# Layer 0's values by seven products of halves, computed a batch ahead, with all experts merged through DRAM and the values' bias carried by the projection

## The chip, the cores and the metric

The kernel runs on one core of a Trainium2 chip. The metric is device time in microseconds (us), from one launch of the whole program. Before the change three runs took 2100.03, 2100.3 and 2100.56 us; the median is 2100.3. The engines are named as in the profile: PE (TensorE, matrix products), DVE (VectorE), ACT (ScalarE), POOL (GpSimd) and SP (SyncE, which here only issues DMAs). Each engine works through its own instructions in order.

## The reference

Two transformer layers in fp32 over x of shape 8 x 512 x 512 (batch, rows, width). What the change touches is the attention and the experts of layer 0 and one step of the attention of layer 1:

```python
# layer 0, attention: 16 heads of 32, causal
q = (x @ WQ_w.T + WQ_b)...; k = (x @ WK_w.T + WK_b)...; v = (x @ WV_w.T + WV_b)...
attn = softmax(where(causal, -inf, q k^T / sqrt(32)))
x = layernorm(x + (attn @ v) @ WO_w.T + WO_b)
# layer 0, experts: 8 experts, the top 2 of a router for each row
gup = x @ gate_up_proj + 2 * (x @ gup_lora_A^T) @ gup_lora_B^T
out = (silu(gate) * h) @ down_proj + 2 * (... @ down_lora_A^T) @ down_lora_B^T
x = layernorm(x + sum over the top 2 of weight * out)
# layer 1, attention: 8 heads of 64 in 2 groups, after an rms norm, not causal
x = layernorm(x + (softmax(q k^T / 8) @ v) @ Wo.T)
# layer 1, a quantised feed-forward layer, and a last layernorm
```

The weights of a softmax's row sum to one, so a constant added to all values of a head comes out of the attention as the same constant. That is why a bias of values can be added after the attention, as WV_b projected by WO_w.

## The kernel before, in words

The stages follow one another on PE: attention of layer 0 from about 5 to 685 us, the experts on tiles of routed rows to about 1060, attention of layer 1 to about 1603, the feed-forward layer to the end. A scheduler sets the order on each engine from its own estimates of durations, except where a stretch is held in the written order.

*Attention of layer 0* (`attention0`) loops over eight batches b of 512 rows. A batch has four groups g of four heads, and a group three units u: key tile 0, key tiles 1 and 3, key tile 2, whose scores are 512, 384 and 128, and 256 columns wide because of the causal mask. So a batch is twelve slots (g, u). In each slot PE makes the scores `sc` (one PSUM tile, so one at a time), then whatever `plan(b)` put into `todo` for the slot, then the weighted values `av` of the slot before (L1542), then the `late` thunks. ACT takes the exponent (L1503) and frees `sc`; POOL masks (L1513); DVE adds the unit to the group's running sum of p (L1550). After a group, PE sums over the keys (`rs`, L1557), ACT makes a first inverse from a logarithm and an exponent (`r_rough`, L78 and L79), DVE refines it (L80, L81) and multiplies (`aoT`, L1564).

The thunks are products of 128 x 512 outputs over four steps of 128, each step written as four pieces of 32 columns (`matmul_by_columns`, L67): the values `ps_v` of the batch itself, four of them in slots (0,0), (0,1) and (0,2), evicted by DVE with the bias added (L1396); the queries `ps_q` and keys `ps_k` of the next group; the projection `ps_o` of the batch before (L1425), its layernorm (L200 to L205), its turn and the router. All of these take PSUM tiles from one pool with two buffers that alternate strictly, so a product can start only when the one before the last has been evicted.

*Turning.* The normalised rows of batch b-1 are transposed in blocks of 32 by DVE (L108), written to DRAM by four stores (L113) and read back as `x1T` by one load (L116), all on SP. Loads that must not get ahead of that return are issued inside `behind_return()`: x of the next batch (L1353), its transpose xT (L1349, into one of two rooms that batches use in turn), and the merged experts' stores (L840) in group 3. SP's queue is in order, and its DMAs share 16 DMA engines. Late in the batch PE makes the router's logits (`score`, `ps_logits`, L515) from x1T; at the start of the next, `choose` (`ps_r`, then a chain of small DVE instructions, L534 to L565) picks the two experts of each row.

*Experts.* Each expert has six tiles of 128 x 512 weights. In unit u = 2 of batches 1 to 6 PE makes LoRA products into the free half of the scores' bank (`deltas`), ACT scales them (`scaled`, L827), and POOL adds them to the weights (`pair`). Experts 0 to 3 are loaded into SBUF at the start and merged there (k below 12, batches 1 to 3). Experts 4 to 7 are merged through DRAM (batches 4 to 6): a load of 256 KB (L837), POOL's add (L839), a store into `merged` (L840). Their room in SBUF holds the attention's weights and xT until the tiles begin; then `load(e)` brings them in.

*Attention of layer 1* forms the inverse of row sums in `normalise` with the same `inverse` (two steps of ACT and two of DVE), 32 times.

## Time and profile before

| what | before |
|---|---|
| median of three runs | 2100.3 us |
| profiled execution, its time | 2100.73 us |
| its span (first to last instruction) | 2098.9 us |
| granted clock of PE | 0.999 |
| PE busy | 2073.1 us (99%) |
| DVE, ACT, POOL busy | 1168.4, 670.6, 515.0 us |
| first scores of batches 0, 1, 2, 3 | 14.87, 82.87, 166.03, 250.50 us |
| first scores of batches 4, 5, 6, 7 | 334.97, 419.45, 503.92, 588.39 us |

In the lines of the profile "L1396 DVE TENSOR_TENSOR v<-ps_v,row" is an instruction of line 1396 on DVE that writes v from ps_v and row. In a timeline the first number is the start, the second the length of a run of equal instructions (x is their count), and in brackets is the idle time before it with what ended that. In a list of waits the numbers are the total, how often, and the longest. In a list of windows the columns are length, busy time of PE, its weight loads, DVE, ACT and POOL, then PE's clock, the share of the DMA engines' time, and GB/s. In a group of instructions they are busy time and mean ns of one, then the idle time before them and its cause. Pieces of a product run partly at the same time, so lengths of PE runs overlap, and the time between two starts is what a run costs.

### The profile page before, as it was taken

Reading aid. Unit: us, or ns where it says so; the run is one execution under the profiler, and the core shown is the slowest. Engines: PE = TensorE matmul, PEld = TensorE weight load, DVE = VectorE, ACT = ScalarE, POOL = GpSimd, SP = SyncE. Lnnn points to the kernel's source line nnn. Section 1 sums busy time; section 2 is a strip of 40 time slices with the busy share of each in tenths; the row PEclk is TensorE's granted clock in tenths of the full one; section 3 lists DMA queues with packets and bytes.
Section 4 is the critical chain, followed back from the end, with each engine's and each line's share of the span. In section 5 each row is a group of like instructions: output and inputs, shape, how many; then the busy total and the mean of one; then the engine's idle time right before and its main releaser. Section 6 shows DMA issues by size and latency. Waiting matters only on the chain. (4 is left out here: it accounts for less than half of the span.)

```text
span 2098.9 us, 36093 instructions
## 1 busy us (share of the span) xinstructions
PE 2073.1 (99%) x15074; PEld 1048.3 (50%) x15074; DVE 1168.4 (56%) x2028; ACT 670.6 (32%) x967; POOL 515.0 (25%) x509
## 2 busy tenths in 40 slices
PE   8999999999999999999999999999999999999998
PEld 2333333333334677774433333333335888888886
DVE  2556666766667633234146677766747644555444
ACT  2433434434434111111143433343332322222222
POOL 1343444434433221221053231323201000000000
PEclk9999999999999999999999999999999999999999
DMA  9011304325233568876431332233102311111000
GB/s 326 22 44 60 101 12 121 117 74 153 82 102 108 173 198 254 245 225 202 149 102 51 121 107 84 71 101 101 41 1 71 101 41 61 61 61 61 20 21 22
DMA packets 182093, 213.42 MB, mean 102 GB/s; under 512 B 72586, under 2 KB 126090, under 8 KB 178850
## 3 DMA queue, kind: packets, MB, share of 16 engines
q1 hardware_dynamic: 169280, 172.85, 26.3%
q0 software_dynamic: 10560, 34.61, 5.7%
q10 hardware_dynamic: 2082, 3.56, 0.6%
q8 instruction: 122, 2.00, 0.4%
q14 instruction: 49, 0.40, 0.1%
HBM read 132.58 MB, written 78.40 MB: 101 GB/s over the span
## 5 line engine op out<-in xcount | busy, mean ns | idle before, releaser
L1503 ACT ACTIVATE p<-sc 128x2048 f32<-128x2048 f32 (+1 forms) x96 | 152.4, 1588 | 157.9 <-PE sc L67 157.9
L1513 POOL TENSOR_SCALAR_AFFINE_SELECT p<-p 128x512 f32<-128x512 f32 x128 | 98.6, 782 | 338.6 <-ACT p L1503 328.0
L1246 DVE SCALAR_TENSOR_TENSOR hT<-ps_u,vec,sg 128x512 f32<-128x512 f32 x88 | 65.5, 745 | 189.6 <-PE ps_u L1241 189.4
L1257 PE MATMUL ps_f<-ffn_w,h_half 128*128 128x512 f32 x664 | 167.7, 393 | 2.7 <-DVE h_half L1252 1.9
L974 PE MATMUL ps_gu<-xrT,experts 128*128 128x256 f32 x736 | 166.6, 379 | 0.0
L1550 DVE TENSOR_TENSOR p<-p 128x1536 f32<-128x1536 f32 (+2 forms) x96 | 144.2, 1503 | 37.5 <-POOL x L1523 31.4
L1094 POOL TENSOR_TENSOR g_total<-g_total,r_inv 128x512 f32<-128x512 f32 x64 | 88.4, 1381 | 291.3 <-DVE r_inv L81 291.3
L974 PEld LDWEIGHTS ps_gu<-xrT,experts 128*128 128x128 f32 x736 | 139.3, 190 | 35.9 <-issue 19.0
L1893 ACT ACTIVATE p<-sc 128x1024 f32<-128x1024 f32 x128 | 124.2, 1016 | 85.6 <-PE sc L67 82.7
L1257 PEld LDWEIGHTS ps_f<-ffn_w,h_half 128*128 128x128 f32 x664 | 122.9, 188 | 34.4 <-DVE h_half L1252 7.3
L1241 PE MATMUL ps_g<-x_high,ffn_w 128*128 128x512 f32 x352 | 137.2, 390 | 0.0
L1241 PE MATMUL ps_g<-x_low,ffn_w 128*128 128x512 f32 x352 | 137.0, 389 | 0.0
L1241 PE MATMUL ps_u<-x_low,ffn_w 128*128 128x512 f32 x352 | 136.9, 389 | 0.0
L1241 PE MATMUL ps_u<-x_high,ffn_w 128*128 128x512 f32 x352 | 136.9, 389 | 0.0
L67 PE MATMUL sc<-qT,kT 64*64 64x512 f32 x1024 | 124.7, 602 | 2.6 <-ACT qT L1784 2.3
L67 PE MATMUL ps_q<-experts 128*32 128x512 f32 x1024 | 121.7, 604 | 5.0 <-DMA experts<-in_xT 4.7
L1244 ACT ACTIVATE sg<-ps_g,vec 128x512 f32<-128x512 f32 x88 | 60.6, 688 | 193.7 <-PE ps_g L1241 193.7
L67 PE MATMUL ps_v<-experts 128*32 128x512 f32 x1024 | 120.9, 595 | 0.0
L1912 PE MATMUL av<-p,v 128*64 128x512 f32 x512 | 120.8, 593 | 0.0
L202 POOL TENSOR_SCALAR rstd<-mv 128x4 f32<-128x4 f32 x15 | 3.9, 260 | 459.0 <-DVE mv L201 459.0
L67 PE MATMUL ps_o<-attn_out,aoT 128*64 128x512 f32 x512 | 116.4, 598 | 0.0
L67 PE MATMUL ps_k<-experts 128*32 128x512 f32 x1024 | 116.3, 594 | 0.0
(284 smaller groups left out, 3329.0 us busy)
## 6 DMA issues: line engine op xcount, KB each, us to landing
results<-y SPq DMA_DIRECT2D x68, 256.0 KB
pair<-xrT SPq DMA_DIRECT2D x30, 512.0 KB
xrT<-pair SPq DMA_DIRECT2D x120, 128.0 KB
turned<-turned SPq DMA_DIRECT2D x56, 256.0 KB
x<-in_x SPq DMA_DIRECT2D x8, 1024.0 KB
rows<-x SPq DMA_DIRECT2D x32, 256.0 KB
experts<-in_xT SPq DMA_DIRECT2D x7, 1024.0 KB
x<-rows SPq DMA_DIRECT2D x14, 512.0 KB
```

The costliest lines, as they stand in the source:

```text
L67: nc.tensor.matmul(out[m], lhsT=lhsT[:, m], rhs=rhs, start=start, stop=stop)
L974: nc.tensor.matmul(ps[:, j, :], lhsT=w, rhs=xT[:, c, :], start=c == 0, stop=c == ND - 1)
L1094: self.nc.gpsimd.tensor_tensor(self.total, self.total, r_inv, ALU.add)
L1241: nc.tensor.matmul(ps, lhsT=w[:, ts(dc, P)], rhs=x[:, dc, :], start=(dc, i) == (0, 0), stop=(dc, i) == (ND - 1, 1))
L1244: nc.scalar.activation(sg, g, AF.Silu, scale=vec[:, V_SG + c : V_SG + c + 1])
L1246: nc.vector.scalar_tensor_tensor(hT, u, vec[:, V_SU + c : V_SU + c + 1], sg, ALU.mult, ALU.mult)
L1257: self.nc.tensor.matmul(os[t], lhsT=h[:, ts(t, P)], rhs=self.weights(2 * NHID + c), start=(c, i) == (0, 0), stop=(c, i) == (NHID - 1, 1))
L1503: nc.scalar.activation(p, sc[:, :, :width], AF.Exp, scale=scale)
L1513: select = nc.gpsimd.affine_select(out=first, in_=first, pattern=[[0, 4], [1, P]], compare_op=ALU.is_ge, fill=0.0, base=0, channel_multipl ...
L1550: nc.vector.tensor_tensor(total[:, :, P * kt :], total[:, :, P * kt :], p[:, :, at : at + w], ALU.add)
L1893: nc.scalar.activation(p, sc, AF.Exp, scale=scale)
L1912: nc.tensor.matmul(st["av"][HD * j : HD * (j + 1), :], lhsT=st["v"][:, kt, HD * j : HD * (j + 1)], rhs=p[:, j, :], start=kt == 0, stop=kt ...
```

## The change

- **Values.** Batch 0 makes its values as before, without the bias. From batch 1 on a batch's 512 x 512 values are made from seven products of 256 x 256 blocks in place of eight (`ps_1of7` to `ps_7of7`, `seven`). This takes sums of blocks of the weights, formed once in batch 0 (`seven_of_weights`), sums of blocks of xT, formed by DVE in each batch (`seven_of_rows`, L806 of the changed kernel), and additions as the products are evicted (L1437 of the changed kernel, one or two per product). Six of the seven are put into slots of the batch before, (1,0) to (3,2), and the last into (0,0) of the batch itself. The values alternate between two rooms in the space of experts 2 and 3.
- **Row sums.** Those of xT(b+1) are in `late` of slots (0,2) and (1,0) of batch b. They read what `load_xT(b+1)` brings.
- **Bias.** `bias_v` is loaded by 4-byte elements, spread by DVE over an identity-shaped tile, projected once by `wo` in batch 0 and added to the row that POOL adds to x.
- **Experts.** All eight are merged through DRAM, in batches 1 to 6; the eight loads of experts 0 to 3 at the start go. Merged experts are loaded in batches 6 and 7, expert 3 after the last weighted values.
- **Layer 1.** `normalise` uses one DVE reciprocal in place of the four steps; a preload of ACT's table between two small activations goes with it.

```diff
--- before.py
+++ after.py
@@ -781,30 +781,49 @@
         return xn, [dev[:, 1, t : t + 1] for t in range(NT)]
 
 
+def seven_of_weights(nc, w, s):
+
+    def block(i, j):
+        return w[:, 2 * j : 2 * (j + 1), 256 * i : 256 * (i + 1)]
+
+    def sums(last):
+        for out, a, b, op in ((block(1, 0), block(0, 0), block(1, 0), ALU.subtract),) if last else (
+                (s[:, 0], block(1, 0), block(1, 1), ALU.add), (s[:, 1], s[:, 0], block(0, 0), ALU.subtract),
+                (s[:, 2], block(0, 1), s[:, 1], ALU.subtract)):
+            nc.vector.tensor_tensor(out, a, b, op)
+
+    return {1: block(0, 0), 2: block(0, 1), 6: s[:, 1], 5: s[:, 0], 7: block(1, 0), 3: s[:, 2], 4: block(1, 1)}, sums
+
+
+def seven_of_rows(nc, xT, t):
+
+    def block(i, j):
+        return xT[:, 2 * i : 2 * (i + 1), 256 * j : 256 * (j + 1)]
+
+    def sums(last):
+        for out, a, b in ((t[3], block(1, 1), block(0, 1)), (t[2], block(1, 0), t[1])) if last else (
+                (t[0], block(0, 1), block(0, 0)), (t[1], block(1, 1), t[0])):
+            nc.vector.tensor_tensor(out, a, b, ALU.subtract)
+
+    return {1: block(0, 0), 2: block(1, 0), 6: t[1], 5: t[0], 7: t[3], 3: block(1, 1), 4: t[2]}, sums
+
+
 class Experts:
 
 
 
     def __init__(self, env, pool, dram):
         self.env, self.nc = env, env.nc
-        self.merged = dram.tile([P, 4, EXPERT], F32, name="merged")
+        self.merged = dram.tile([P, E, EXPERT], F32, name="merged")
         self.w = pool.tile([P, E * EXPERT], F32, name="experts")
         self.by_expert = self.w.rearrange("p (e f) -> p e f", f=EXPERT)
 
-    def room(self, i):
-
-        at = 4 * EXPERT + i * ND * 512
-        return self.w[:, at : at + ND * 512].rearrange("p (u f) -> p u f", f=512)
+    def room(self, at, n):
+
+        return self.w[:, at : at + n * 512].rearrange("p (u f) -> p u f", f=512)
 
     def load(self, e):
-        at = e * EXPERT
-        if e >= 4:
-            self.nc.sync.dma_start(out=self.by_expert[:, e, :], in_=self.merged[:, e - 4, :])
-            return
-        for src, n in ((self.env.ins.gate_up[e], ND), (self.env.ins.down[e], UPS - ND)):
-            self.nc.sync.dma_start(out=self.w[:, at : at + n * 512].rearrange("p (u f) -> p u f", f=512),
-                                   in_=src.rearrange("u p f -> p u f"))
-            at += n * 512
+        self.nc.sync.dma_start(out=self.by_expert[:, e, :], in_=self.merged[:, e, :])
 
     def load_lora(self, pool, i):
 
@@ -825,15 +844,12 @@
         e, f = 2 * i, slice(512 * c + 256 * half, 512 * c + 256 * (half + 1))
         scaled = own.tile([P, 2, 256], F32, tag=f"scaled{i}", name="scaled")
         nc.scalar.mul(scaled, ps[:, e : e + 2, :], LORA_SCALE)
-        if not second:
-            w = self.by_expert[:, e : e + 2, f]
-            return {1 + i: lambda: nc.gpsimd.tensor_tensor(w, w, scaled, ALU.add)}
-        w = []
+        w, e = [], 4 * second + e
 
         def load():
             w.append(own.tile([P, 2, 256], F32, tag=f"merged{i}", name="merged"))
             ins, u = self.env.ins, c if c < ND else c - ND
-            src = (ins.gate_up if c < ND else ins.down)[4 + e : 6 + e, u, :, 256 * half : 256 * (half + 1)]
+            src = (ins.gate_up if c < ND else ins.down)[e : e + 2, u, :, 256 * half : 256 * (half + 1)]
             nc.sync.dma_start(out=w[0], in_=src.rearrange("e p f -> p e f"))
 
         return {0: load, 1 + i: lambda: nc.gpsimd.tensor_tensor(w[0], w[0], scaled, ALU.add),
@@ -1324,6 +1340,7 @@
     HD = 32
     scale = 1.0 / math.sqrt(HD)
     UNITS = ((0,), (1, 3), (2,))
+    ORDER = 1, 6, 2, 5, 3, 7, 4
     with ExitStack() as phase:
         work = phase.enter_context(tc.tile_pool(name="a_work", bufs=1))
         small = phase.enter_context(tc.tile_pool(name="a_small", bufs=2))
@@ -1334,14 +1351,21 @@
 
 
         nc.scalar.preload_act_table_set(EXP_AND_LN)
-        wv, wq, wk, wo = (experts.room(i) for i in (0, 2, 3, 5))
+        wv, x_odd, wq, wk, x_even, wo = (experts.room(4 * EXPERT + ND * 512 * i, ND) for i in range(6))
+        v_rooms = [experts.room(i * EXPERT, ND) for i in (2, 3)]
+
+        def quarters(at, n):
+            return experts.w[:, at : at + n * 512].rearrange("p (s u f) -> p s u f", s=n, f=256)
+
+        sv, t_x, t_last = (quarters(at, n) for at, n in ((EXPERT, 3), (EXPERT + 1536, 3), (2 * EXPERT + ND * 512, 1)))
+        t_x = [*(t_x[:, i] for i in range(3)), t_last[:, 0]]
 
         def load_w(room, i, units=slice(0, ND)):
             src = ins.w_attn0[ND * i + units.start : ND * i + units.stop]
             nc.sync.dma_start(out=room[:, units, :], in_=src.rearrange("u p f -> p u f"))
 
         def load_xT(b):
-            xts[b] = experts.room((1, 4)[b % 2])
+            xts[b] = (x_odd, x_even)[b % 2]
             if b == 0:
                 for c in range(ND):
                     nc.sync.dma_start(out=xts[b][:, c, :], in_=ins.xT[b][ts(c, P), :])
@@ -1363,6 +1387,8 @@
         nc.sync.dma_start(out=row, in_=ins.rows.partition_broadcast(P))
         load_w(wq, 1, others)
         load_w(wk, 2, others)
+        bias_v = own.tile([P, ND], F32, name="bias_v")
+        nc.sync.dma_start(out=bias_v, in_=ins.rows[0].rearrange("(c p) -> p c", p=P))
         router = Router(env, keep, routes, small, work, dram)
         router.load()
         load_x(0)
@@ -1372,13 +1398,10 @@
             nc.sync.dma_start(out=router.results[ts(i, P), :], in_=guard.total)
         load_w(wo, 3)
         experts.load_lora(work, 0)
-        for e in range(4):
-            experts.load(e)
 
         ones = own.tile([P, HD], F32, name="ones")
         nc.gpsimd.memset(ones, 1.0)
 
-        vs = [None] * NT
         heads = {}
         aoTs = {}
 
@@ -1392,8 +1415,55 @@
             ps = mm([P, D], "ps_v")
             for c in range(ND):
                 multiply(ps, xts[b][:, c, ts(t, P)], wv[:, c, :], c)
-            vs[t] = own.tile([P, D], F32, tag=f"v{t}", name=f"v{t}")
-            nc.vector.tensor_tensor(vs[t], ps, row[:, 0, :], ALU.add)
+            nc.vector.tensor_copy(v_rooms[b % 2][:, t, :], ps)
+
+        v_of, v_sums = seven_of_weights(nc, wv, sv)
+
+        def row_sums(b):
+            return seven_of_rows(nc, xts[b], t_x)
+
+        def seven(b, n):
+            x_of, _ = row_sums(b)
+            room = v_rooms[b % 2]
+            ps = mm([P, 2, 256], f"ps_{n}of7")
+            for s in range(2):
+                for k in range(2):
+                    matmul_by_columns(nc, ps[:, s, :], x_of[n][:, k, ts(s, P)], v_of[n][:, k, :], start=k == 0, stop=k == 1)
+
+            def block(i, j):
+                return room[:, 2 * j : 2 * (j + 1), 256 * i : 256 * (i + 1)]
+
+            def add(out, a):
+                nc.vector.tensor_tensor(out, ps, a, ALU.add)
+
+            if n == 1:
+                nc.scalar.copy(block(0, 0), ps)
+            elif n == 6:
+                add(block(1, 0), block(0, 0))
+            elif n == 2:
+                add(block(0, 0), block(0, 0))
+            elif n == 5:
+                add(block(1, 1), block(1, 0))
+            elif n == 3:
+                add(block(0, 1), block(1, 1))
+            elif n == 7:
+                add(block(1, 1), block(1, 1))
+                add(block(1, 0), block(1, 0))
+            else:
+                add(block(1, 0), block(1, 0))
+
+        spread = []
+
+        def spread_bias():
+            spread.append(work.tile([P, ND, P], F32, tag="logits", name="spread"))
+            for c in range(ND):
+                nc.vector.tensor_scalar(spread[0][:, c, :], env.ident, 0.0, bias_v[:, c : c + 1], ALU.mult, ALU.add)
+
+        def out_of_bias():
+            ps = mm([P, D], "ps_bias")
+            for c in range(ND):
+                multiply(ps, spread[0][:, c, :], wo[:, c, :], c)
+            nc.vector.tensor_tensor(row[:, 1, :], ps, row[:, 1, :], ALU.add)
 
         def query(b, g):
             ps = mm([P, S], "ps_q")
@@ -1540,7 +1610,7 @@
                 w = S - P * kt
                 for j in range(4):
                     nc.tensor.matmul(av[HD * j : HD * (j + 1), P * kt :],
-                                     lhsT=vs[kt][:, P * g + HD * j : P * g + HD * (j + 1)], rhs=p[:, j, at : at + w],
+                                     lhsT=v_rooms[b % 2][:, kt, P * g + HD * j : P * g + HD * (j + 1)], rhs=p[:, j, at : at + w],
                                      start=u == 0, stop=kt == UNITS[-1][-1])
                 at += w
             at = 0
@@ -1577,8 +1647,14 @@
         def plan(b):
 
             todo, late = ({(g, u): [] for g in range(ND) for u in range(len(UNITS))} for _ in range(2))
-            for slot, places in (((0, 0), (0, 1)), ((0, 1), (3,)), ((0, 2), (2,))):
-                todo[slot] += [lambda t=t: value(b, t) for t in places]
+            if b == 0:
+                for slot, places in (((0, 0), (0, 1)), ((0, 1), (3,)), ((0, 2), (2,))):
+                    todo[slot] += [lambda t=t: value(b, t) for t in places]
+                late[1, 0] += [lambda: v_sums(False), spread_bias]
+                todo[1, 1].append(out_of_bias)
+                late[1, 1].append(lambda: v_sums(True))
+            else:
+                todo[0, 0].append(lambda: seven(b, ORDER[-1]))
             pb, last = b - 1, b == NB - 1
             by_dma = 0 <= pb < by_blocks
             for g in range(ND):
@@ -1601,6 +1677,12 @@
                     todo[(3, 0) if last else (2, 2)].append(lambda: choose(pb))
             if b == 0:
                 todo[1, 0].append(lambda: router.merge_lora(mm([P, ND, E], "ps_wr")))
+            if b + 1 < NB:
+                for slot, last_sums in (((0, 2), False), ((1, 0), True)) if b else (((2, 1), False), ((2, 2), True)):
+                    late[slot].append(lambda last_sums=last_sums: row_sums(b + 1)[1](last_sums))
+                for n, slot in zip(ORDER, ((1, 0), (2, 0), (2, 2), (3, 0), (3, 1), (3, 2)) if b else
+                                   ((3, 0), (3, 0), (3, 1), (3, 1), (3, 2), (3, 2))):
+                    todo[slot].append(lambda n=n: seven(b + 1, n))
             if b > 1:
                 todo[0, 0].append(lambda: choose(b - 2, mm=aside))
                 todo[1, 0].append(lambda: dispatch(b - 2))
@@ -1649,8 +1731,12 @@
                         load_x(b + 1)
                 if b == NB // 2 and g == 0:
                     experts.load_lora(work, 1)
+                if b == NB - 2 and g == 1:
+                    with behind_return():
+                        experts.load(0)
                 if b == NB - 1 and g == 1:
-                    experts.load(4)
+                    for e in (1, 2, 4):
+                        experts.load(e)
                 if b == NB - 1 and g == 2:
                     order.enter_context(in_order(tc))
                 if b == NB - 1 and g == 3:
@@ -1672,6 +1758,7 @@
                 summing = lambda b=b, g=g, acc=acc: normalise(b, g, acc)
         waiting()
         summing()
+        experts.load(3)
         heads_ctx.close()
         tiles.open(tiles_ctx)
         tiles.open_rows()
@@ -1839,12 +1926,9 @@
 
         def prepare_table(function):
             out = work.tile([P, 2, S], F32, tag="p", name="p1_none", bufs=4)
-            return nc.scalar.activation(out[:, 0, :1], env.neg_half[:, :1], function)
-
-        with env.tc.issue_after(prepare_table(AF.Copy).ins):
-            preload = nc.scalar.preload_act_table_set(EXP_AND_LN)
-        with env.tc.issue_after(preload.ins):
-            prepare_table(AF.Exp)
+            nc.scalar.activation(out[:, 0, :1], env.neg_half[:, :1], function)
+
+        prepare_table(AF.Exp)
 
         small = env.small
         pieces = {0: self.first}
@@ -1920,7 +2004,7 @@
                 nc.tensor.matmul(rs[HD * j : HD * (j + 1), :], lhsT=ones, rhs=total[:, j, :], start=True, stop=True)
             r_inv = work.tile([P, S], F32, tag="r_inv", name="r_inv1")
             guard.watch_sums(rs, r_inv)
-            inverse(nc, r_inv, rs, work.tile([P, S], F32, tag="r_rough", name="r_rough1"))
+            nc.vector.reciprocal(r_inv, r_inv)
             ao = state[b]["aoT"][:, g, :]
             if b != self.BY_TENSOR:
 

```

## The prediction

> **What bounds the kernel now.** I read the page first (busy shares and the slices), then what TensorE (PE) waited for, then the stretches, and then the timelines of PE, SP, DMA, GpSimd (POOL) and VectorE (DVE) around the turn from one batch of layer 0 to the next. The page:

> ```profile
> PE 2073.1 (99%) x15074; PEld 1048.3 (50%) x15074; DVE 1168.4 (56%) x2028; ACT 670.6 (32%) x967; POOL 515.0 (25%) x509
> PEclk9999999999999999999999999999999999999999
> ```

> PE is the bound at full clock (0.999). Its longest waits, and columns for one early-merge batch (SBUF), one later batch (merged by way of DRAM) and attention of layer 1:

> ```profile
> PE ps_q L67 <- DMA experts<-in_xT: 4.7, 1, 4.7
> PE sc L67 <- ACT qT L1784: 2.3, 1, 2.3
> PE ps_f L1257 <- DVE h_half L1252: 1.9, 7, 0.5
> ```

> ```profile
> 250.50:334.97 84.47, 84.33 (x1080) 28.08 (x1080) 55.25 (x110) 33.94 (x44) 37.33 (x36) 1.00 0.22 67
> 419.45:503.92 84.47, 84.33 (x1080) 28.08 (x1080) 55.25 (x110) 33.93 (x44) 36.40 (x36) 1.00 0.37 115
> 1060.00:1603.00 543.00, 539.59 (x3271) 181.83 (x3269) 365.25 (x511) 213.26 (x315) 152.75 (x132) 1.00 0.25 75
> ```

> PE work removed is time gained, and any new wait of PE is time lost. The two batches last equally long with either way of merging.

> **The change part by part.** All by the profiled execution (2100.73 us; the median is 2100.3, 0.4 less, so I add the sum to the median).

> *Seven products.* The prices come from PE's timeline at the turn from batch 4 to batch 5, counted from 0 (start, length):

> ```profile
> 405.15 3.64 PE L67 MATMUL ps_q<-experts 128*32 128x512 f32 x32
> 408.60 0.61 PE L1542 MATMUL av<-p,v 128*32 128x256 f32 x8
> 409.15 1.12 PE L67 MATMUL sc<-q,k 32*64 32x384 f32 x32
> 410.20 3.64 PE L67 MATMUL ps_k<-experts 128*32 128x512 f32 x32
> 413.65 1.04 PE L1542 MATMUL av<-p,v 128*32 128x512 f32 x8
> 414.51 1.04 PE L1557 MATMUL rs<-p,ones 128*32 128x512 f32 x8
> 415.49 0.69 PE L67 MATMUL sc<-lora 16*64 16x256 f32 x16
> ```

> By starts, a full product (ps_q; ps_v is the same form) takes 3.45, four steps of 0.86. A step of 512 columns is 0.86 where the next has the same tile shape (413.65 to 414.51) and 0.98 where it changes (to 415.49), so a change of shape is 0.12. The step of 256 columns takes 0.55 with a change: 0.43. Half the width is half the time, and 0.55 is no bound, because a seventh follows and precedes products of its own shape. A seventh is four such steps, 1.72. Seven are 12.05 against 4 x 3.45 = 13.8: -1.72 a batch, batches 1 to 7. Batch 0 keeps its four values.

> *A small stall filled.* The first scores of a batch (419.45 here) wait for ACT's second `scaled` to read the scores' bank; it ended at 334.92 a batch earlier, the scores began at 334.97. PE's last weighted values would have let them begin 1.03 earlier. The last seventh now stands there: -1.03 more. So a batch without new stalls is 84.47 - 2.75 = 81.72.

> *Unstalled sum.* From the start of batch 0's scores to batch 1's, 68.0 us: + 3.45 (bias through the projection, one product) + 6 x 1.72 (sevenths of batch 1) - 0.9 (its own filled stall) = +12.9. Batch 1: -2.8. Batches 2 to 6: 5 x -2.75 = -13.75. Batch 7 drops 13.8 and keeps one seventh: -12.07; its queries then follow a choose chain on DVE, +1.25. Together -14.5.

> *The new wait.* This decides. The row sums of x(b+2) need its load, and DVE works in order. The order of the built kernel puts two of those sums (L806, the first waiting for that load's semaphore) on DVE right behind the eviction of product 5, and ahead of product 3's eviction, the sums of p, r_inv, aoT, products 7 and 4 and the whole choose chain, in each of the turns 1 to 2 up to 5 to 6. Before, nothing waited early for xT. SP issues the load behind x1T's return, x and two stores:

> ```profile
> 409.50 0.33 SPq L116 DMA_DIRECT2D x1T<-turned  x1
> 409.92 0.39 SPq L1353 DMA_DIRECT2D x<-in_x  x1
> 410.37 1.37 SPq L840 DMA_DIRECT2D merged<-merged  x2
> 411.78 0.48 SPq L1349 DMA_DIRECT2D experts<-in_xT  x1
> ```

> and the 16 DMA engines, in 40 slices of 404 to 426 us, are full until about 423.5:

> ```profile
> DMA  9899989710094599898699799999999999600000
> ```

> The load's last semaphore update is at 423.43, 13.9 after x1T's issue (13.4 a batch later; 11.6 to 11.7 in batches without stores, which now all have them). Call the start of the last group's scores, 404.10, zero. Before, x1T was issued at +5.4; products 6 and 2 move in front and take 3.44 of PE from after to before that point, while 6's eviction (0.65) delays the normalised rows, so it comes 2.8 to 3.1 earlier: +2.3. POOL's merges (3.50, ending before the stores) still fit. The load lands at L = +15.8 (15.3 to 16.7, from 13.4 to 13.9 and the two issue offsets). DVE reaches it at +7.15 (scores 1.05, the query product 3.45, product 5 1.72, and 0.93 until that is evicted: 0.69 and the lag seen on others). It waits 8.6.

> Queued behind, after L: two sums and product 3's eviction (3 x 0.69), done at L+2.1; p, r_inv, aoT, p at L+8.1; 7 (twice), 4, two row sums at L+11.4; the choose chain, 6.08 here:

> ```profile
> 428.23 0.18 DVE L534 TENSOR_REDUCE red<-ps_r 128x4 f32<-128x32 f32 x1
> 434.91 0.68 DVE L1396 TENSOR_TENSOR v<-ps_v,row 128x512 f32<-128x512 f32 x1
> 436.43 0.75 DVE L1407 TENSOR_SCALAR q<-ps_q,vec 128x512 f32<-128x512 f32 x1 [0.84 <-PE ps_q L67]
> ```

> then q's eviction, which ends at L+18.7. The two PSUM buffers of the products alternate: ps_logits needs product 3 evicted (L+2.2 against PE's arrival at +15.87, so 2.1), and the next ps_k needs q evicted (against +30.48, so L+18.75-30.48 = L-11.7). The first stall is contained in the second. At L = 15.8 that is 4.1, with POOL and DVE slowing each other up to 4.6: 4.3, range 3.4 to 5.5. Were xT never late, DVE's own chain would still cost 1.3. Five turns: 5 x 4.3 = +21.5. In turn 0 to 1 xT lands at 72 to 75, its sums come at 85: nothing.

> [...]

> *More DVE work.* Four evictions become seven plus four row sums: +7 x 0.69 = 4.8 on 55.25 of 84.47 busy. Its cover is that idle time; its cost where the cover is gone is in the chain above. ACT gets a copy of 0.6 on 33.9: nothing.

> *Merging all by DRAM.* 24 more loads and stores on SP and DMA (share 0.22 to 0.37, as later batches have). The equal 84.47 says 0, bar the 2 us later landing, already in L. Eight start loads (6 MB) go, so xT(1) is issued near 21 and not 36 us: nothing waits for it. The last loads of merged experts lie 37 us ahead of first use, landing in about 8: 0.

> *bias_v.* 512 packets of 4 bytes ahead of the router's loads, against r_wr (512 of 32 bytes), landed 14.7 to 16.5. DVE's spread waits for it near 16, the first value's eviction is due at 19.6: 0, up to 1 if it lands later; below 0 no row allows.

> *Attention of layer 1.* ACT's two steps and DVE's two become one reciprocal:

> ```profile
> L80 DVE SCALAR_TENSOR_TENSOR r_inv<-r_inv,r_rough 128x512 f32<-128x512 f32 x63 | 43.6, 692 | 117.6 <-ACT r_rough L79 116.7
> L1561 DVE RECIPROCAL r_inv<-r_inv 128x512 f32<-128x512 f32 x1 | 3.3, 3340 | 0.0
> ```

> DVE: 3.34 - 0.69 - 0.73 = +1.92, 32 times, 61 on 365.25 of 543. It starts 1.2 earlier, as DVE idles 1.87 a time for ACT's r_rough. aoT comes 0.7 later where DVE is idle, 1.9 where it is dense; the projection reads it a group or more later. Bounds 0 and 8 x 0.69 = 5.5 (one exposed per batch); I take 0. The table switch is reordered, its total kept: 0.

> Sum: -14.5 + 21.5 = **+7.0, 2107.3**.

> **The rivals.**
> 1. *xT is in time* (issued earlier or moved faster than the rows have it). [...] Against: engines full from 410 to 423.5. L below 13 gives s = 1.3: -14.5 + 6.5 = -8, **2092.3**, faster. It decides at s = 2.9, L = 14.4 to 14.6.
> 2. *Half late*, L about 14.4, s = 2.7: -14.5 + 13.5 = -1, **2099.3**, no difference.
> 3. *The reciprocal binds in layer 1.* For: 26.91 of the 30 us from 1266 to 1296 are busy on DVE. Against: 67% over the stage. +5.5 on the forecast: **2112.8**.

> **How the numbers follow.** Forecast 0.5 (s of 3.4 to 5.5 gives 2102.5 to 2113.3), rival 1 0.2, rival 2 0.17, rival 3 0.13. Measurement tells 0.2%, 4.2 us. Faster is rival 1 with the edge of 2: 0.21; same is 2 and the forecast's low edge: 0.20; slower the rest: 0.59. The range cuts a tenth at each end: 2091 to 2115.

> **What the profile would show.** Right: DVE waits of about 8 us five times for experts<-in_xT at the row sums; PE waiting for DVE at ps_logits and ps_k about 2 each in five batches; batches of 86 us in place of 84.5; 49 sevenths of 1.72; no wait of PE in layer 1 that leads to the 32 reciprocals of 3.34. Wrong: batches near 82 to 83 (xT in time), a seventh above 1.8, or waits of ps_o for aoT after 1060 us.

## The result

The changed kernel takes 2114.61 us (median of five runs, 2111.25 to 2119.06) against 2100.48 (2100.03 to 2101.4): slower by a factor of 1.0069, 95% interval 1.005 to 1.0087. The forecast was slower, at 2107.3 with a range of 2091 to 2115. The sign and the mechanism came true; the loss is twice the forecast, +14.1 for +7.0.

### The profile after

PE's longest waits in the changed kernel. The first two lines are new:

```profile
PE ps_k L67 <- DVE q L1477: 16.0, 6, 3.3
PE ps_logits L515 <- DVE experts L1437: 6.6, 5, 2.1
PE ps_q L67 <- DMA experts<-in_xT: 4.4, 1, 4.4
```

22.6 us of waiting for DVE, where the prediction summed five stalls of 4.3 and one of 1.25 to 22.75. What holds DVE, in its own list of waits:

```profile
DVE experts L806 <- DMA experts<-in_xT: 40.2, 5, 8.8
```

Five waits of 8.0 on average (8.6 predicted). The turn from batch 4 to 5 on the three engines, SP first, then DVE (the row sums, product 3, the queries' eviction), then PE:

```profile
418.79 0.33 SPq L116 DMA_DIRECT2D x1T<-turned  x1
419.22 1.22 SPq L1377 DMA_DIRECT2D x<-in_x  x1
420.49 1.02 SPq L856 DMA_DIRECT2D merged<-merged  x2
421.55 0.54 SPq L1373 DMA_DIRECT2D experts<-in_xT  x1
```

```profile
433.33 1.42 DVE L806 TENSOR_TENSOR experts<-experts 128x512 f32<-128x512 f32 x2 [8.14 <-DMA experts<-in_xT]
434.67 0.68 DVE L1437 TENSOR_TENSOR experts<-ps_3of,experts 128x512 f32<-128x512 f32 x1
...
452.59 0.74 DVE L1477 TENSOR_SCALAR q<-ps_q,vec 128x512 f32<-128x512 f32 x1
```

```profile
435.40 1.06 PE L515 MATMUL ps_logits<-x1T,r_wr 128*32 128x512 f32 x8 [1.43 <-DVE experts L1437]
436.29 1.91 PE L67 MATMUL ps_7of<-experts 128*32 128x256 f32 x32
...
453.38 5.34 PE L67 MATMUL ps_k<-experts 128*32 128x512 f32 x32 [3.27 <-DVE q L1477]
458.53 1.05 PE L1612 MATMUL av<-p,experts 128*32 128x384 f32 x16
```

The last group's scores start at 418.02. x1T is issued 0.8 later (2.3 predicted), xT's load lands 15.3 later (15.8 predicted; the profile has its last semaphore update at 433.31), and the sums start at once. The query's eviction ends at +35.3, and ps_k starts there. So far the mechanism is the predicted one. The new thing stands in the third and fourth line: ps_k, a full product, takes 5.15 from start to start and not 3.45. PE's granted clock in the windows around it:

```profile
450.87:454.28 3.41, 0.90 (x11) 0.30 (x15) 3.21 (x10) 2.04 (x4) 0.64 (x1) 1.00 0.00 0
454.28:457.70 3.42, 3.42 (x24) 0.86 (x20) 3.25 (x5) 0.00 (x0) 0.44 (x1) 0.50 0.01 2
457.70:461.11 3.41, 3.41 (x52) 1.10 (x48) 1.93 (x2) 1.05 (x2) 3.41 (x3) 1.00 0.02 5
```

For 3.41 us PE runs at half clock, right behind a stretch in which it was busy for only 0.90 us, and loses half of that, 1.7 us. The profile has four such stretches, from 174.39, 276.79, 365.54 and 454.29, beside one behind PE's last work, which every profile here has; the profile before has none but that. Two whole batches, 5 and 6, show the price:

```profile
438.99:527.08 88.09, 83.60 (x1180) 31.29 (x1177) 59.81 (x117) 34.43 (x44) 37.75 (x34) 0.98 0.39 127
527.08:612.18 85.10, 81.83 (x1180) 30.96 (x1177) 59.97 (x117) 34.43 (x44) 37.91 (x35) 1.00 0.34 101
```

Batch 6 is 81.83 of work and one wait of 3.27. Batch 5 has waits of 3.27 and 1.22, makes 86.32 so far, and takes 88.09: 1.77 more, at a mean clock of 0.98.

Where the 13.9 us between the two profiled spans (2112.8 and 2098.9) come from, by batches of layer 0 (from first scores to first scores; batch 7 to the first product of the tiles):

| batch | 0 | 1 | 2 | 3 | 4 | 5 | 6 | 7 |
|---|---|---|---|---|---|---|---|---|
| before | 68.01 | 83.16 | 84.47 | 84.47 | 84.47 | 84.47 | 84.47 | 80.51 |
| after | 80.95 | 84.27 | 83.96 | 87.84 | 88.29 | 88.09 | 85.10 | 70.12 |
| difference | +12.9 | +1.1 | -0.5 | +3.4 | +3.8 | +3.6 | +0.6 | -10.4 |

They sum to +14.6; the rest of the span gives back 0.7. The waits for DVE in turns 1 to 2 up to 5 to 6 are 2.08, 0.66, 1.22, 1.43 and 1.22 at ps_logits, and 1.40 and then four times 3.27 at ps_k.

### The profile page after: what moved, and what is told of

The parts are those of the page before. It is cut to its first block, busy times and chain, and to the rows that moved or that the text cites. A ratio compares the mean times of both kernels' runs of the same rounds, so it can differ in the third digit from the quotient of the medians.

```text
span 2112.8 us, 37546 instructions
## 1 busy us (share of the span) xinstructions
PE 2065.7 (98%) x15778; PEld 1070.4 (51%) x15778; DVE 1264.5 (60%) x2054; ACT 642.1 (30%) x909; POOL 511.9 (24%) x509
## 3 DMA queue, kind: packets, MB, share of 16 engines
q1 hardware_dynamic: 180240, 185.44, 27.9%
q8 instruction: 127, 2.08, 0.4%
## 5 line engine op out<-in xcount | busy, mean ns | idle before, releaser
L1110 POOL TENSOR_TENSOR g_total<-g_total,r_inv 128x512 f32<-128x512 f32 x64 | 83.7, 1307 | 321.5 <-DVE r_inv L2007 270.7
L2007 DVE RECIPROCAL r_inv<-r_inv 128x512 f32<-128x512 f32 x32 | 107.1, 3347 | 72.8 <-ACT r_inv L1107 72.8
L1257 PE MATMUL ps_g<-x_high,ffn_w 128*128 128x512 f32 x352 | 137.2, 390 | 0.0
L1257 PE MATMUL ps_g<-x_low,ffn_w 128*128 128x512 f32 x352 | 137.0, 389 | 0.0
L1257 PE MATMUL ps_u<-x_high,ffn_w 128*128 128x512 f32 x352 | 137.0, 389 | 0.0
L1257 PE MATMUL ps_u<-x_low,ffn_w 128*128 128x512 f32 x352 | 136.9, 389 | 0.0
L67 PE MATMUL ps_k<-experts 128*32 128x512 f32 x1024 | 121.3, 616 | 16.0 <-DVE q L1477 16.0
L67 PE MATMUL sc<-qT,kT 64*64 64x512 f32 x1024 | 124.7, 602 | 1.2 <-ACT qT L1871 0.9
L67 PE MATMUL ps_q<-experts 128*32 128x512 f32 x1024 | 119.7, 601 | 4.7 <-DMA experts<-in_xT 4.4
L67 PE MATMUL ps_o<-attn_out,aoT 128*64 128x512 f32 x512 | 116.4, 598 | 0.0
L67 PE MATMUL ps_q<-hT,attn_qkv 128*64 128x512 f32 (+1 forms) x504 | 116.2, 596 | 0.0
```

The lines of the kernel that those rows point to most:

```text
L67: nc.tensor.matmul(out[m], lhsT=lhsT[:, m], rhs=rhs, start=start, stop=stop)
L1110: self.nc.gpsimd.tensor_tensor(self.total, self.total, r_inv, ALU.add)
L1257: nc.tensor.matmul(ps, lhsT=w[:, ts(dc, P)], rhs=x[:, dc, :], start=(dc, i) == (0, 0), stop=(dc, i) == (ND - 1, 1))
L2007: nc.vector.reciprocal(r_inv, r_inv)
```

## The experiments

The theory: row sums that wait on DVE for xT's late load stall PE, and PE's idling then halves its clock for a stretch. The rivals: DVE has simply too much work, the place of the sums is bad whenever xT lands, or another edit (reciprocals, merging through DRAM) costs.

### 1. Row sums behind the query's eviction

```diff
+        def late_sums(b, last_sums):
+            with tc.issue_after(evicted[b, 1].ins) if b else ExitStack():
+                row_sums(b + 1)[1](last_sums)
...
-    late[slot].append(lambda last_sums=last_sums: row_sums(b + 1)[1](last_sums))
+    late[slot].append(lambda last_sums=last_sums: late_sums(b, last_sums))
```

Here `evicted[b, 1]` is the DVE instruction that evicts the queries of group 1.

> The changed kernel with one edit: DVE's row sums of xT(b+1) are issued behind the eviction of the batch's second query, so nothing on DVE waits early for xT. Theory (the lost time is the wait for xT and the half-clock stretches that follow PE's idling): no DVE wait for experts<-in_xT, no PE wait at ps_logits for DVE, ps_k waits under 1 us each, granted clock 0.999 in place of 0.995; batches of about 82 us and 2100.5 - 14.5 + 0 to 1.3, that is 2085 to 2088. Rival (DVE simply has too much work now, 71% of a batch): the same work stands behind the query and holds up the sums of p instead; the time stays above 2105.

Measured: 2087.18 us, ratio to the kernel before 0.9936 (0.992 to 0.9953). PE's waits, where the query's line is left once (batch 7) and the logits' line is gone, and two batches:

```profile
PE ps_q L67 <- DMA experts<-in_xT: 4.3, 1, 4.3
PE ps_f L1273 <- DVE h_half L1268: 2.0, 7, 0.5
PE ps_k L67 <- DVE q L1477: 1.5, 1, 1.5
```

```profile
340.08:421.93 81.85, 81.84 (x1181) 30.98 (x1177) 58.93 (x117) 34.54 (x44) 37.15 (x35) 1.00 0.37 118
421.93:503.77 81.84, 81.84 (x1181) 30.97 (x1177) 58.95 (x117) 34.52 (x44) 37.20 (x35) 1.00 0.42 137
```

DVE does almost the same work in a batch (58.9 us for 59.8 to 60.0), and PE does not wait for it in these batches; there is no half-clock stretch but the one behind PE's last work. The rival of too much DVE work falls. 27.4 us lie between this kernel and the changed one: 21.1 of waits (22.6 - 1.5) and 6.8 of clock make 27.9. This version beats both kernels.

### 2. xT ahead of x on SP

```diff
-                if g == (0 if b else 2) and b + 1 < NB:
-                    with behind_return():
-                        load_xT(b + 1)
+                if (b, g) == (0, 2):
+                    load_xT(1)
+                if g == 3 and b + 2 < NB:
+                    with behind_return():
+                        load_xT(b + 2)
                 if g == 3 and b + 1 < NB:
                     with behind_return():
                         load_x(b + 1)
```

> The changed kernel with one edit: xT two batches ahead is loaded right behind the return of x1T, in front of x and of the merged experts' stores on SP's queue; the row sums keep their early place on DVE. Theory: xT lands near 11 us after the last group's scores in place of 16, the DVE wait shrinks from 8 to about 4 us, ps_logits no longer waits, ps_k waits about the floor of 1.3, no half-clock stretch; 2091 to 2094. Rival (the place of the sums on DVE is the cost whenever xT lands): ps_k still waits 3 us and more, 2105 or above.

Measured: 2091.39 us, ratio 0.9959 (0.9945 to 0.9973). DVE's wait for the load and PE's for DVE:

```profile
DVE experts L806 <- DMA experts<-in_xT: 10.7, 5, 3.0
```

```profile
PE ps_k L67 <- DVE q L1477: 6.0, 6, 1.5
```

The sums stand in the same early place, and DVE waits 2.1 on average for xT (4 were expected). So 1 MB and two stores fewer ahead of xT turn the loss of 14 us into a gain of 9. The waits at ps_k are 0.9 each in five batches (the floor was estimated at 1.3) and 1.5 in batch 7; the clock stays full (0.999). So it was the load's landing, not the place alone.

### 3. The reciprocals of layer 1 alone

```diff
-            inverse(nc, r_inv, rs, work.tile([P, S], F32, tag="r_rough", name="r_rough1"))
+            nc.vector.reciprocal(r_inv, r_inv)
...
-        with env.tc.issue_after(prepare_table(AF.Copy).ins):
-            preload = nc.scalar.preload_act_table_set(EXP_AND_LN)
-        with env.tc.issue_after(preload.ins):
-            prepare_table(AF.Exp)
+        prepare_table(AF.Exp)
```

on the kernel before.

> The kernel before with the changes of layer 1 alone (one DVE reciprocal in place of four steps, no preload between the small activations). Theory: DVE gets 61 us more work in the stage and PE none of it: 2099 to 2102. Rival (the reciprocals are part of the lost time): 2104 to 2110.

Measured: 2099.71 us, ratio 0.9997 (0.9987 to 1.0006): no difference. The DVE work, 62 us more over the program (1230.7 for 1168.4), lies beside PE's. A small gain was missed: without the preload's place in the order ACT loads its table (1.28) while PE still makes the first queries, and no longer behind them, and PE's wait at the first scores shrinks from 2.28 to 0.86:

```profile
1064.79 1.95 PE L67 MATMUL sc<-qT,kT 64*64 64x512 f32 x16 [2.28 <-ACT qT L1784]
```

```profile
1063.12 1.95 PE L67 MATMUL sc<-qT,kT 64*64 64x512 f32 x16 [0.86 <-ACT qT L1784]
```

The first line is of the kernel before, the second of this one.

### 4. Four products again, all else as changed

```diff
-            if b == 0:
+            if True:
                 for slot, places in (((0, 0), (0, 1)), ((0, 1), (3,)), ((0, 2), (2,))):
                     todo[slot] += [lambda t=t: value(b, t) for t in places]
...
-                for n, slot in zip(ORDER, ...):
-                    todo[slot].append(lambda n=n: seven(b + 1, n))
```

The sums of weights and of rows go as well.

> The changed kernel with the values by four products in the batch itself, as before the change; no row sums, no weight sums; all experts still merged through DRAM, bias still through the projection, reciprocals as changed. Theory: only the bias's one product is added, 2100.5 + 3.5 = 2104, within 1.5; no half-clock stretch, batches of 84.5. Rival (merging all experts through DRAM costs by its transfers or POOL's waits): 2107 or more, with batches 1 to 3 longer than 84.5.

Measured: 2106.6 us, ratio 1.0025 (1.0014 to 1.0036), 1.1 above the upper end of the theory's 1.5 and below the rival's 2107. The rival's sign, longer batches, is absent: batches 1 to 6 last as before.

```profile
337.93:422.40 84.47, 84.32 (x1080) 28.08 (x1081) 55.25 (x110) 33.96 (x44) 36.40 (x35) 1.00 0.44 136
```

Layer 0's attention takes 657.48 from first scores to tiles, against 654.03: +3.45, the bias's one product. The rest lies in the tiles, 388.56 against 385.14, where PE waits 1.8 for a returned pair and 1.0 for fetched rows. The changed kernel itself has no such waits there (385.59). Why this one has was not tried, so whether they come from merging all experts through DRAM stays open.

### 5. PE made to wait in the kernel before

These five kernels have nothing of the change. In batches 2 to 6 DVE makes idle reciprocals ahead of the eviction of the second query:

```diff
+                for n in (512, 512) if g == 1 and 1 < b < NB - 1 else ():
+                    nc.vector.reciprocal(q[:, :n], ps[:, :n])
                 nc.vector.tensor_scalar(q, ps, vec[:, V_BQ + g : V_BQ + g + 1], None, ALU.add)
```

with widths (256,), (512,), (512, 256), (512, 512) and (512, 512, 512).

> The kernel before, with nothing of the change: in batches 2 to 6 DVE makes one idle reciprocal of half a tile (1.7 us) ahead of the eviction of the second query, so that PE waits at the next ps_k. The output is unchanged, the extra work is overwritten. Theory (a short idle time of PE costs itself, a long one a half-clock stretch too): five waits of about 1.5 us, clock 1.0 throughout, 2108. Rival (the clock drops for another reason than PE's idling): the same here.

> The kernel before with one idle reciprocal of a whole tile (3.3 us) there. Theory: five waits of about 3.2 us, as long as those of the changed kernel after which the clock was halved; 16 us of waiting, and some of the five followed by a half-clock stretch of 3.41 us at 1.7 us lost each: 2116.5 to 2125. Rival: 2116.5 and full clock.

> The kernel before with one and a half idle reciprocals there. Theory: five waits of about 5.6 us, 28 us of waiting, and most of the five followed by a half-clock stretch: 2132 to 2137. Rival: 2128.5 and full clock.

Measured: 2103.66 (ratio 1.0015, 1.0005 to 1.0025), 2103.75 (1.0017, 1.0007 to 1.0026) and 2110.79 (1.0051, 1.0034 to 1.0068). All three expectations missed, because a value's product stands ahead of that ps_k in PE's real order and covers 3.45 us more: the first two leave no wait at ps_k at all, the third waits of 1.3. They settle nothing about the batches. But in both of the first two a half-clock stretch stands at another place, the wait for ACT ahead of layer 1's first scores, in the same form. Its 1.7 us and five new waits of 0.3 for r_rough make 3.2 of the 3.3 and 3.1 us by which their spans are longer. The windows of the first of them:

```profile
1063.03:1066.44 3.41, 1.13 (x7) 0.30 (x9) 0.00 (x0) 2.17 (x4) 1.15 (x3) 1.00 0.00 0
1066.44:1069.85 3.41, 3.41 (x20) 1.00 (x20) 0.00 (x0) 1.02 (x1) 2.80 (x3) 0.50 0.66 175
```

The kernel before has the same wait of 2.28 us at the same place, spread over two windows, and keeps full clock:

```profile
1060.72:1064.13 3.41, 1.78 (x5) 0.47 (x3) 0.00 (x0) 1.48 (x2) 0.64 (x2) 1.00 0.17 63
1064.13:1067.50 3.37, 2.43 (x21) 0.72 (x24) 0.00 (x0) 2.25 (x5) 2.46 (x4) 1.00 0.47 129
```

So stronger doses were taken.

> The kernel before with two idle reciprocals of a whole tile ahead of the second query's eviction in batches 2 to 6, since the smaller doses left PE idle for 1.3 us at most. Theory: five idle times of about 3.0 us, costing 5 x 3.6 = 18 with what r_rough holds up; where one of the clock's fixed windows of 3.41 us lies idle for 2 us or more, the next window is at half clock and 1.7 us are lost: 1 to 5 such windows, 2120 to 2127, and none after a window idle for under 1.9 us. Rival (a half-clock stretch needs PE idle for longer than 3.4 us, or has nothing to do with idling): full clock in the five batches, 2118.5.

> The kernel before with three idle reciprocals there. Theory: five idle times of about 7 us, 5 x 7.4 = 37; every one contains a window of 3.41 us that is idle for 2 us or more, so a half-clock stretch follows each of the five, partly within the idle time itself: 2138 to 2146. Rival (no tie between idling and the clock): 2137.5 and full clock.

Measured: 2124.02 (ratio 1.0105, 1.0088 to 1.0122) and 2147.4 (1.0218, 1.0201 to 1.0235). The waits are 2.2 and 5.8 us, not 3.0 and 7.0. The first lies in the range of the theory: 18 for the five batches (88.06 without a stretch for 84.47, so 3.6 each, as reckoned, though the waits are 2.5 of it and PE's busy time, 85.40 for 84.33, the rest, whose cause is not shown), three stretches in the batches and one ahead of layer 1's first scores, 6.8, make 24.8 for the 25.0 between the spans. The second lies 1.4 above its range, which was reckoned from 2100.5, where the kernel before took 2102.22 beside these two. It has five half-clock stretches of two windows each, 6.83 us, and one of a single window ahead of layer 1's first scores. In the weaker of the two three of five equal waits are followed by one, and two are not. Windows of the weaker kernel, one of each kind:

```profile
456.45:459.86 3.41, 1.44 (x10) 0.22 (x2) 3.41 (x3) 0.00 (x0) 2.08 (x2) 1.00 0.33 117
459.86:463.27 3.41, 3.17 (x32) 1.07 (x36) 3.31 (x6) 0.00 (x0) 1.29 (x1) 1.00 0.73 196
545.20:548.61 3.41, 1.20 (x10) 0.21 (x9) 3.41 (x4) 0.00 (x0) 1.40 (x2) 1.00 0.44 154
548.61:552.02 3.41, 3.41 (x20) 0.85 (x16) 3.23 (x5) 0.00 (x0) 1.28 (x1) 0.50 0.57 154
```

The same wait of 2.21 us falls into one window in the second case (idle 3.41 - 1.20 = 2.21; half clock follows) and over the edge of one in the first (1.97; none follows). The starts of the half-clock stretches lie whole multiples of 3.413 us apart (30, 26 and 26 windows in the changed kernel; 28 and 241 between the starts at 193.34, 288.91 and 1111.52 in the kernel with three reciprocals), so the windows stand fixed and the work moves against them. In both kernels of the change, with the windows laid on that grid, and in the windows shown here of the five kernels with idle reciprocals, every window idle for 2.04 us or more is followed by half clock, and no window at full clock that is idle for 1.97 or less is. (This leaves out what lies before the first record of the clock, 9.4 us into the kernel before and 7.1 into the changed one.) The window of 2.04 (3.41 - 1.37) stands in the kernel with three reciprocals, ahead of layer 1's first scores:

```profile
1108.11:1111.52 3.41, 1.37 (x4) 0.30 (x2) 0.00 (x0) 1.89 (x3) 1.05 (x2) 1.00 0.04 16
1111.52:1114.94 3.42, 3.18 (x16) 0.85 (x20) 0.00 (x0) 1.31 (x3) 2.51 (x4) 0.50 0.55 157
```

The changed kernel's one wait of 3.27 that no half clock follows is spread over two windows, idle for 1.41 and 1.85:

```profile
536.21:539.62 3.41, 2.00 (x44) 0.62 (x36) 3.20 (x14) 2.45 (x6) 2.52 (x3) 1.00 0.23 81
539.62:543.03 3.41, 1.56 (x16) 0.55 (x20) 3.31 (x6) 1.39 (x3) 0.64 (x1) 1.00 0.03 5
```

For a window that is itself at half clock the limit is not shown. In the kernel with three reciprocals such a window idle for 0.92 us is followed by another at half clock, and in the changed kernel full clock comes back after one idle for 0.46 (276.79 to 280.20, where PE is busy for 2.95). A limit between the two would fit, from one case on each side. The case of 0.92, with the two windows in one line:

```profile
288.91:295.74 6.83, 5.91 (x28) 1.38 (x32) 3.88 (x6) 0.00 (x0) 1.27 (x1) 0.50 0.01 2
```

In the kernel with two reciprocals, batches without a stretch take 88.06, with one 89.76: 1.70.

## Why the prediction was right in its sign and short by half

- **The seven products.** Right. 1.72 each by the starts (436.29 to 438.01), and 81.85 for a batch in experiment 1, 81.72 predicted. Batch 0's +12.9 is exact, and batch 7's -10.4 stands for -12.07 + 1.25 = -10.8.
- **The new wait.** Right in place and cause, and in total size: 22.6 us of stalls for 22.75. That the total fits so well is partly luck, as errors cancel. The landing was 15.3 for 15.8: x1T was issued at +0.8 and not +2.3, and xT's load took 14.5 from there and not 13.4 to 13.9. In the turn 4 to 5 the query's eviction then ended 20.0 after the landing and not 18.7. The choose chain is 6.68 long by the rows that the prediction shows (428.23 to 434.91) and not 6.08, and the sum of 18.7 agrees with 6.68. The split is off too: about 2 each were forecast at ps_logits and ps_k, and four of the five turns have 0.66 to 1.43 and 3.27, so the single idle times were longer than thought. That POOL and DVE slow each other shows in the turn 4 to 5: a row sum takes 0.69 at 433.33, with POOL idle, and 1.81 at 443.01, beside POOL's merges, and the two merges from 440.77 take 3.50, where in the kernel before the two from 383.84 take 2.51. Rivals 1 and 2, a load in time, did not happen, and experiment 2 shows the sum for it: 2091.39 where rival 1 was worked out to 2092.3.
- **The unstalled sum.** -14.5 was 1.2 too good: in experiment 1, which has only the stall of batch 7 left (1.5 for the 1.25 in that sum), layer 0's attention takes 640.75 from first scores to tiles against 654.03, so -13.3. About half of the difference is the batch of 81.85 in place of 81.72, five times. The rest is mostly batch 7.
- **What failed** is the sum's last step, "-14.5 + 21.5 = +7.0". It priced a stall at its own length. The working had read the granted clock as 0.999 throughout and had no term for what an idle PE does to it. Four half-clock stretches at 1.7 are 6.8. By what was measured, -13.3 + 21.1 + 6.8 = +14.6, the sum of the table. That +7.0 + 6.8 = +13.8 lies as near to the 13.9 between the spans is luck in the decimals: +1.2, -0.4 and -0.7 cancel. Why the five runs lie 8 us apart, where those of before lie within 1.4, is not shown. A stall more or less over the edge of a window would move a run by 1.7, and the slowest run has the lowest granted clock (0.994) and one of the two fastest the highest (0.997). But the runs of 2111.25 and 2118.32 both have 0.995, so the clock explains at most a part.
- **Layer 1.** Rival 3 did not happen (experiment 3); the table switch was priced at 0 and gave 1.4. The changed kernel has one new wait of 0.9 for DVE's sums behind a reciprocal, at 1103 us, which experiments 1 to 3 do not have.
- **The range of the forecast.** s, the stall of one turn, of 3.4 gives -14.5 + 17.0, so 2102.8 and not 2102.5.
- **Merging through DRAM and bias_v** cost nothing that shows in layer 0's attention: experiment 4 has the batches unchanged, and +3.45 in all, the bias's one product. The 2.8 of waits in its tiles stay open.

## What to carry to other kernels

An operation that needs a late load should not be issued ahead of short evictions on the same engine, even if its result is wanted much later: a wait of 8.14 us at a row sum held up all that stood behind it on DVE, and moving four row sums behind one eviction was worth 27 us here, more than the arithmetic saved. Before a wait is put into the sum, compare it with the clock's windows of 3.41 us: here stalls of PE of 2.08 to 3.27 us cost 1.7 us on top in some cases (three of five at 2.21, three of four at 3.27), whether PE waited for DVE, as in layer 0, or for ACT, as ahead of layer 1's first scores (2.28). And a forecast that finds a stall of several us should look for a cheap reordering that removes it, since the same profile lines name it.
